# An LSTM cell updated in two halves, and the eigenvector work given out by window length

## The chip, the cores and the metric

The kernel runs on one core of a Trainium2 chip. The metric is the device time of one execution in microseconds; the time before is the median of three runs. The profile is one separately profiled execution of the same program. The engines are named as in the profile: PE (matmuls), PEld (weight loads for PE), DVE (vector), ACT (activations), POOL (general), SP (which here issues most transfers).

## The reference, cut to what matters

Four graph layers run one after the other over `x` of shape (128, 64, 256): 128 batches, 64 nodes, 256 features. After each layer comes a residual and a layer norm. The change concerns the first layer and, through the work that is interleaved with it, the eigenvectors for the fourth.

```python
# layer 0
h = relu(einsum('ts,bsh->bth', adj, x @ Wg0 + bg0))
h = relu(einsum('ts,bsh->bth', adj, h @ Wg1 + bg1))
for p in range(1, 5):
    nw = Tv // p                                   # Tv = 64 nodes
    wins = h[:, :nw * p, :].reshape(Bv * nw, p, Hd)
    last = lstm_last(Wih[p-1], Whh[p-1], bih[p-1], bhh[p-1], wins)
    h = h.at[:, arange(nw) * p + (p - 1), :].set(last.reshape(Bv, nw, Hd))
x = layernorm(x + h)

# one LSTM step, gates in the order i, f, g, o, zero initial state
g = x_t @ Wih.T + h @ Whh.T + bias
c = sigmoid(f) * c + sigmoid(i) * tanh(gg)
h = sigmoid(o) * tanh(c)

# layer 3 needs U
_, U = eigh(L_norm)        # 64x64, from adj
```

Windows of p nodes in a row are run through an LSTM of p steps; the last hidden state replaces the last node of each window. This is done for p = 1, 2, 3 and 4 in turn, each on the result of the one before. The eigenvectors `U` depend on `adj` alone, so they can be computed at any time before layer 3.

## The kernel before, in words

Everything is fp32. In the first layer the batches are split into four groups (`g`), each of 16 tiles of two batches (`TG = 16`). A group's state `H` holds the features on the 128 partitions in two halves (the index `c`), and 2048 columns (two batches by 64 nodes by 16 tiles).

For each group the loop at L1649 runs `windows` for p = 1, 2, 3, 4. In `windows` (L1564) the columns are cut into parts: four for p = 1 (512 columns each), two for p = 2 (512), two for p = 3 (336), one for p = 4 (512). For each part the p steps run in order (`k`). In a step the gates come in the order 0, 1, 3, 2, that is i, f, o, g; f is left out in the first step, when the old cell is zero. Each gate has two chunks `c`, the two halves of the hidden features. A chunk is two matmuls from `H` with the input weights `wi` (L1589) and, from the second step on, two from the hidden state `hst`, tile `lh`, with `wh` (L1593). Both add up in one of four PSUM banks (tag `pq`). ACT then applies the sigmoid or tanh with the bias and writes the chunk into the gate's tile (L1595). In the trace each matmul call is two PE instructions.

Only when all gates are done is the cell updated, on both chunks at once, with operations of 1024 columns (672 for p = 3): the product of i and g at L1605 (L1603 in a first step), the product of the old cell and f at L1606, their sum at L1607, the tanh of the cell on ACT at L1608, and the product with o, which is the new `lh`, at L1611. In the last step the product is written straight into `H` instead, by two strided operations (L1615). The next step's L1593 needs `lh`; the next p needs `H`.

Three kinds of work are interleaved. `side` issues parts of something else on PE: the residual and layer norm of the group before while p is 1 and 2, and the graph convolution of the group after while p is 3 and 4. `pump` issues pieces of the eigenvector computation, mostly chains of tiny DVE operations on 64 rows, a few with 64x64 matmuls. Each call adds an amount of units to what is owed and takes pieces off a generator until it is paid; a piece says what it is worth, 1.1 to 5 units, or 2.6 where it doesn't say. A piece is tied behind the DVE instruction that was written down last, so that it can't be put ahead of it in DVE's queue:

```python
with tc.issue_after(mark[0]):
    while owed[0] > 0:
        owed[0] -= next(pieces, None) or 2.6
```

Within a step `pump` is called after each chunk but the last two (L1597). The amount is 1.2 (a first step) or 2.13 (a later one), times the columns over 512, times `PACE`, 1.9. What is left of the pieces is pumped beside the second layer and must be done before the third begins.

Each engine works through its own queue in order. The order of the queues is set when the program is built: a scheduler takes the instructions by their place in the program and by when it reckons that their operands will be ready, so a queue isn't always in the order of the code. The small matrix `b0w` is made once at the start from a bias, and read by four PE instructions (L1520).

Of the kernel before, what the change touches and what calls it, by code (L numbers as in the profile page):

```python
# [7 lines left out]
F32 = mybir.dt.float32  # L8
I32 = mybir.dt.int32
AF = mybir.ActivationFunctionType  # L10
ALU = mybir.AluOpType
# [6 lines left out]
P = 128  # L18
# [1241 lines left out]
def tile_adj_resnorm(ctx: ExitStack, tc: tile.TileContext, I: dict, out: bass.AP, layers: int = 4):  # L1260
    nc = tc.nc
    v, s, te = nc.vector, nc.scalar, nc.tensor
# [18 lines left out]
    lh = head.enter_context(tc.tile_pool(name="lh", bufs=1, side="right"))  # L1281
# [99 lines left out]
    PACE = 1.9  # L1381

    def pump(n):

        owed[0] += n
        body = nc.cur_bb.bb.instructions
        for i in reversed(body[seen[0] :]):
            if i.engine == mark[0].engine:
                mark[0] = i
                break  # L1390
# [3 lines that stand above are left out]
        seen[0] = len(body)  # L1394
# [84 lines left out]
    with tc.tile_pool(name="lw", bufs=1) as lw, tc.tile_pool(  # L1479
        name="l0c", bufs=1  # L1480
    ) as lc, tc.tile_pool(name="l0p", bufs=2, space=PSUM) as pp, tc.tile_pool(
        name="l0r", bufs=1, space=PSUM
    ) as pr, tc.tile_pool(name="l0q", bufs=4, space=PSUM) as pq:
        G = 4 * D
        TG = 16
# [19 lines left out]


        negc = lw.tile([P, 2, N], F32, tag="negc", name="negc")
        b0w = lw.tile([P, 2, P], F32, tag="b0w", name="b0w")
        rs = lw.tile([P, 1], F32, tag="rs", name="rs")
        ps = pp.tile([P, 512], F32, tag="ps", name="ps")  # L1510
        te.matmul(ps[:, :P], ones, bda, start=True, stop=True)
# [52 lines left out]
        def windows(l0, H, p, w, side):  # L1564


            wi, wh = w
            nw = N // p
            hn = H.rearrange("p c (b n j) -> p c b n j", b=2, j=TG)

            parts = {1: [(b, b + 1, n, n + 32) for b in range(2) for n in (0, 32)], 4: [(0, 2, 0, nw)]}.get(
                p, [(b, b + 1, 0, nw) for b in range(2)])
            for b0, b1, n0, n1 in parts:
                M = (b1 - b0) * (n1 - n0) * TG
                at = lambda c, k: hn[:, c, b0:b1, n0 * p + k : (n1 - 1) * p + k + 1 : p, :]
                cst_ = l0.tile([P, 2, 512], F32, tag="lc", name="lc", bufs=2)
                hst = None
                for k in range(p):
                    gates, left = {}, 8 if k else 6
                    for gt in (0, 1, 3, 2):  # L1580
                        if gt == 1 and k == 0:
                            continue
                        gates[gt] = l0.tile([P, 2, 512], F32, tag="gate", name="gate", bufs=5)
                        for c in range(2):
                            left -= 1
                            o = gt * 2 + c
                            ps = pq.tile([P, 512], F32, tag="pq", name="pq")[:, :M]
                            for kk in range(2):
                                te.matmul(ps, wi[:, kk, o * P : (o + 1) * P], at(kk, k),  # L1589
                                          start=(kk == 0), stop=(k == 0 and kk == 1))  # L1590
                            if k:
                                for kk in range(2):
                                    te.matmul(ps, wh[:, kk, o * P : (o + 1) * P], hst[:, kk, :M],  # L1593
                                              start=False, stop=(kk == 1))
                            s.activation(gates[gt][:, c, :M], ps, AF.Tanh if gt == 2 else AF.Sigmoid,  # L1595
                                         bias=bl[:, p - 1, o : o + 1])
                            if left >= 2:  # L1597
                                pump((0.8 * 6 / 4 if k == 0 else 1.6 * 8 / 6) * M / 512 * PACE)
                            side(M / 512 * (1 if k == 0 else 2))
                    cs2 = cst_[:, :, :M]  # L1600
                    gi, gg, go = (gates[q][:, :, :M] for q in (0, 2, 3))
                    if k == 0:
                        v.tensor_tensor(cs2, gi, gg, ALU.mult)  # L1603
                    else:
                        v.tensor_tensor(gi, gi, gg, ALU.mult)  # L1605
                        v.tensor_tensor(cs2, cs2, gates[1][:, :, :M], ALU.mult)  # L1606
                        v.tensor_tensor(cs2, cs2, gi, ALU.add)  # L1607
                    s.activation(gg, cs2, AF.Tanh)  # L1608
                    if k < p - 1:
                        hst = l0.tile([P, 2, 512], F32, tag="lh", name="lh")  # L1610
                        v.tensor_tensor(hst[:, :, :M], go, gg, ALU.mult)  # L1611
                    else:
                        wb = lambda a, c: a[:, c, :].rearrange("p (b w j) -> p b w j", w=n1 - n0, j=TG)
                        for c in range(2):
                            v.tensor_tensor(at(c, k), wb(go, c), wb(gg, c), ALU.mult)  # L1615

        def residual(g, H, pool, tag):
            hj = H.rearrange("p c (m j) -> p c j m", j=TG)
# [28 lines left out]
        with tc.tile_pool(name="l0g", bufs=1) as l0:  # L1647
            back = iter(())
            for g in range(NT // TG):  # L1649


                side = paced(back, TG // 2, LOAD[1] + LOAD[2] - 4)
                for p in (1, 2):
                    windows(l0, H, p, weights(p), side)
                for _ in back:
                    pass
                last, more = H, iter(())
                if g < NT // TG - 1:
                    if g < NT // TG - 2:
                        load_x(g + 2)  # L1660
                    H = new_h(g + 1)
                    more = convolve(g + 1, H)
                side = paced(more, TG * 2, LOAD[3] + LOAD[4] - 4)
                for p in (3, 4):
                    windows(l0, last, p, weights(p), side)
                for _ in more:
                    pass
                if g < NT // TG - 1:
                    back = residual(g, last, pr, "pr")
# [16 lines left out]
    lw, sm = own2(only1, name="l1w", bufs=1), own2(only1, name="l1s", bufs=2)  # L1686
# [42 lines left out]
    for q in range(NQ):  # L1729
        nc.sync.dma_start(xd[q], xq(q))  # L1730
        at = sm.tile([P, 2, 512], F32, tag="at", name="at")
# [71 lines left out]
    with tc.tile_pool(name="eps3", bufs=1, space=PSUM) as eps:  # L1803
# [7 lines left out]
        with tc.For_i(0, nc.values_load(again[0:1, 0:1], min_val=0, max_val=1)):  # L1811
            with tc.tile_pool(name="gk2", bufs=1) as gk2, tc.tile_pool(name="gt2", bufs=1) as gt2, tc.tile_pool(
                name="gp2", bufs=1, space=PSUM
# [9 lines left out]
    with ExitStack() as l2:  # L1823
# [215 lines left out]
        lw, sm = own1(valuing, name="l2w", bufs=1), own1(valuing, name="l2s", bufs=2)  # L2039
# [17 lines left out]
        with tc.tile_pool(name="l3w", bufs=1) as l3w, tc.tile_pool(name="l3s", bufs=2) as s3, tc.tile_pool(  # L2057
            name="l3p", bufs=6, space=PSUM
# [144 lines left out]
```

## Time and profile before

| what | value |
|---|---|
| median of 3 runs | 2417.96 us (2417.39 to 2418.26) |
| the profiled execution | 2424.67 us |
| its span, first to last instruction | 2422.9 us |
| mean granted PE clock | 0.98 |
| first layer's gate matmuls | from 71.5 us to 1528 us |
| DVE busy in the whole span | 1791.2 us |
| ACT busy in the whole span | 961.6 us |

The span is what the profile accounts for; the execution's own time has 1.8 us more around it, and the profiled execution is 6.7 us above the median of the runs.

A row of the groups reads: line, engine, operation, the tile written and the tiles read, partitions x columns, how often; then the busy time in us and the mean of one in ns; then the idle time of that engine just before these instructions, with what ended it. A matmul's end is modelled and overlaps the next one's start, so a busy PE is not PE at its peak. PEclk is the granted clock as a share of full speed. A line of the timeline begins with its start and its duration in us. A line of the table of stages has the stretch, its length, busy time and number of instructions, the granted clock, and the DMA engines' share and GB/s.

### The profile page before, as it was taken

The numbers are of one execution on the slowest core, as the hardware profiler recorded it, in microseconds if no ns is written. First come the engines' busy times: TensorE is split into PE (matmuls) and PEld (weight loads), VectorE is DVE, ScalarE is ACT, GpSimd is POOL, SyncE is SP. The second block draws the span as 40 slices with busy tenths as digits, with TensorE's granted clock in tenths as the row PEclk, the third lists the DMA queues.
The fourth block names the chain that finished last, engine by engine and source line by source line (L and its number), as shares of the span: only waits on it lengthen the run. The fifth ranks groups of instructions, "written<-read, shape, count | busy, mean of one in ns | idle before, by whom it ended". The sixth has DMA issues, their size and how long they took to land. (4 is left out here: it accounts for less than half of the span.)

```text
span 2422.9 us, 29207 instructions
## 1 busy us (share of the span) xinstructions
PE 2291.4 (95%) x9016; PEld 1228.3 (51%) x9016; DVE 1791.2 (74%) x8172; ACT 961.6 (40%) x1678; POOL 76.2 (3%) x115
## 2 busy tenths in 40 slices
PE   7999999999999999999999989998989999899797
PEld 5544654444565444664444554554433433246786
DVE  4667766677977788867799887687867878457577
ACT  2322322242323242333242322333437875456575
POOL 0000000000000000000000000000000000002331
PEclk9999999999999999999999999999999999899899
DMA  6001000000100010100000100012211000511622
GB/s 217 18 18 35 1 35 1 25 28 18 53 1 35 1 53 18 52 2 34 35 18 18 53 18 18 1 66 87 78 45 35 27 22 26 96 40 43 136 88 75
DMA packets 59859, 101.24 MB, mean 42 GB/s; under 512 B 5136, under 2 KB 40080, under 8 KB 59440
## 3 DMA queue, kind: packets, MB, share of 16 engines
q1 hardware_dynamic: 54624, 88.83, 11.6%
q0 software_dynamic: 3216, 10.21, 1.5%
q8 instruction: 72, 1.18, 0.2%
q14 instruction: 91, 0.75, 0.1%
q10 hardware_dynamic: 1856, 0.28, 0.1%
HBM read 67.84 MB, written 31.46 MB: 41 GB/s over the span
## 5 line engine op out<-in xcount | busy, mean ns | idle before, releaser
L1589 PE MATMUL pq<-H,wi 128*128 128x512 f32 (+1 forms) x2016 | 829.7, 547 | 6.0 <-DVE H L1615 5.1
L1595 ACT ACTIVATE gate<-pq,bl 128x512 f32<-128x512 f32 (+1 forms) x504 | 317.3, 635 | 848.9 <-PE pq L1593 668.6
L1589 PEld LDWEIGHTS pq<-H,wi 128*128 128x128 f32 x2016 | 373.8, 191 | 334.5 <-issue 260.0
L1593 PE MATMUL pq<-lh,wh 128*128 128x512 f32 (+1 forms) x1152 | 477.2, 540 | 25.7 <-DVE lh L1611 25.3
L1593 PEld LDWEIGHTS pq<-lh,wh 128*128 128x128 f32 x1152 | 216.1, 192 | 224.0 <-issue 138.3
L1928 DVE SCALAR_TENSOR_TENSOR xs<-xs 128x512 f32<-128x512 f32 x256 | 165.3, 682 | 64.8 <-ACT xs L1927 63.8
L1927 ACT COPY xs<-l 128x512 f32<-128x512 f32 x256 | 136.7, 586 | 76.0 <-PE l L1920 38.9
L1920 PE MATMUL l<-edge_s,xq 64*128 64x512 f32 x512 | 136.1, 630 | 17.6 <-ACT xs L1927 12.7
L1897 PE MATMUL m<-wqv,xT 128*128 128x512 f32 x256 | 122.7, 616 | 0.8 <-DVE xT L1888 0.8
L1741 PE MATMUL ps<-at,w 128*128 128x512 f32 x256 | 116.7, 607 | 4.1 <-ACT at L1737 3.6
L1759 PE MATMUL ps<-h,w 128*128 128x512 f32 x256 | 113.6, 602 | 6.9 <-ACT h L1754 6.9
L1608 ACT ACTIVATE gate<-lc 128x1024 f32<-128x1024 f32 (+1 forms) x72 | 69.0, 958 | 123.2 <-DVE lc L1603 62.8
L1253 ACT ACTIVATE X<-X,ln_sh,ln_rs 128x256 f32<-128x256 f32 x192 | 99.2, 590 | 19.5 <-DVE ln_sh L1249 13.8
L142 DVE COPY AQR<-eps 64x192 f32<-64x192 f32 (+1 forms) x125 | 35.1, 281 | 94.0 <-PE eps L148 93.9
L1237 DVE BATCH_NORM_STATS2 ln_st<-X 128x6 f32<-128x256 f32 x256 | 99.2, 415 | 2.2
L1605 DVE TENSOR_TENSOR gate<-gate 128x1024 f32<-128x1024 f32 (+1 forms) x36 | 38.0, 1056 | 73.2 <-ACT gate L1595 73.2
L1897 PEld LDWEIGHTS m<-wqv,xT 128*128 128x128 f32 x256 | 46.0, 193 | 77.6 <-issue 62.9
L1759 PEld LDWEIGHTS ps<-h,w 128*128 128x128 f32 x256 | 48.6, 193 | 66.6 <-issue 56.6
L1920 PEld LDWEIGHTS l<-edge_s,xq 64*128 64x128 f32 x512 | 46.4, 190 | 70.0 <-issue 33.0
L1992 POOL DMA_DIRECT2D xr<-xv x32 | 17.6, 549 | 2018.5 <-PE m L1897 1804.3
L1741 PEld LDWEIGHTS ps<-at,w 128*128 128x128 f32 x256 | 47.1, 192 | 60.0 <-issue 47.2
L1874 PE MATMUL sc<-xs,az 128*32 128x512 f32 x512 | 69.1, 612 | 3.1 <-DVE xs L1928 3.1
(556 smaller groups left out, 3217.9 us busy)
## 6 DMA issues: line engine op xcount, KB each, us to landing
wi<-in_WihT_dram SPq DMA_DIRECT2D x16, 1024.0 KB, 4.9
wh<-in_WhhT_dram SPq DMA_DIRECT2D x12, 1024.0 KB, 6.4
X<-in_x_dram SPq DMA_DIRECT2D x16, 512.0 KB, 8.8
xd<-X SPq DMA_DIRECT2D x16, 512.0 KB, 4.0
X<-xd SPq DMA_DIRECT2D x16, 512.0 KB, 3.2
xv<-xv SPq DMA_DIRECT2D x32, 256.0 KB, 2.0
xr<-xv POOLq DMA_DIRECT2D x32, 256.0 KB, 2.9
M<-attn_d SPq DMA_DIRECT2D x16, 512.0 KB, 11.2
```

The lines of the kernel that those rows point to most:

```text
L1237: nc.vector.bn_stats(st, self.X[:, k, :])
L1253: nc.scalar.activation(x, x, AF.Identity, bias=sh[:, k : k + 1], scale=rs[:, k : k + 1])
L1589: te.matmul(ps, wi[:, kk, o * P : (o + 1) * P], at(kk, k), start=(kk == 0), stop=(k == 0 and kk == 1))
L1593: te.matmul(ps, wh[:, kk, o * P : (o + 1) * P], hst[:, kk, :M], start=False, stop=(kk == 1))
L1595: s.activation(gates[gt][:, c, :M], ps, AF.Tanh if gt == 2 else AF.Sigmoid, bias=bl[:, p - 1, o : o + 1])
L1741: te.matmul(ps, w1[:, k, c * P : (c + 1) * P], at[:, k, :], start=(k == 0), stop=(k == 1))
L1759: te.matmul(ps, w2[:, k, c * P : (c + 1) * P], h[:, k, :], start=(k == 0), stop=(k == 3))
L1874: mms.append(te.matmul(sc[half][c][q : q + 32, :], az[:, c, HU - 1 - u_ : 3 * HU - 1 - u_], xs[b, i], start=(u_ == 0), stop=(u_ == HU - 1)))
L1897: te.matmul(ps, xT[:, i, c, :], wqv[:, c, :], start=(c == 0), stop=(c == 1))
L1920: mms.append(te.matmul(pl[i][:, b, :], xq[i][r, c * P : (c + 1) * P], GG[r, :], start=True, stop=True))
L1927: taken.append(s.copy(x, pl[i][:, b, :]))
L1928: ready.append(v.scalar_tensor_tensor(x, x, 0.2, x, ALU.mult, ALU.max))
```

## The change

The cell is updated chunk by chunk inside the loop over gates. After each chunk of gate f the product with the old cell is issued; after each chunk of gate g, which is the last, the product of i and g, the sum, the tanh and, but in the last step, the product into the hidden state. The hidden state's tile is taken at the start of the step and has two buffers. The two operations into `H` stand behind the loop over the steps and are the same as before.

The pump's amount is multiplied by 0.85 for p = 1 and 2, and by 1.1 for p = 3 and 4. `b0w` no longer has a place of its own, but takes that of `h1`, a tile of the convolution.

```diff
-        b0w = lw.tile([P, 2, P], F32, tag="b0w", name="b0w")
+        b0w = lc.tile([P, 2, 512], F32, tag="h1", name="b0w")[:, :, :P]
...
                 for k in range(p):
+                    hnew = l0.tile([P, 2, 512], F32, tag="lh", name="lh", bufs=2) if k < p - 1 else None
                     gates, left = {}, 8 if k else 6
...
                             if left >= 2:
-                                pump((0.8 * 6 / 4 if k == 0 else 1.6 * 8 / 6) * M / 512 * PACE)
+                                pump((0.8 * 6 / 4 if k == 0 else 1.6 * 8 / 6) * M / 512 * PACE * (0.85 if p < 3 else 1.1))
                             side(M / 512 * (1 if k == 0 else 2))
-                    cs2 = cst_[:, :, :M]
-                    gi, gg, go = (gates[q][:, :, :M] for q in (0, 2, 3))
-                    if k == 0:
-                        v.tensor_tensor(cs2, gi, gg, ALU.mult)
-                    else:
-                        v.tensor_tensor(gi, gi, gg, ALU.mult)
-                        v.tensor_tensor(cs2, cs2, gates[1][:, :, :M], ALU.mult)
-                        v.tensor_tensor(cs2, cs2, gi, ALU.add)
-                    s.activation(gg, cs2, AF.Tanh)
-                    if k < p - 1:
-                        hst = l0.tile([P, 2, 512], F32, tag="lh", name="lh")
-                        v.tensor_tensor(hst[:, :, :M], go, gg, ALU.mult)
-                    else:
-                        wb = lambda a, c: a[:, c, :].rearrange("p (b w j) -> p b w j", w=n1 - n0, j=TG)
-                        for c in range(2):
-                            v.tensor_tensor(at(c, k), wb(go, c), wb(gg, c), ALU.mult)
+                            cs, g = cst_[:, c, :M], {q: a[:, c, :M] for q, a in gates.items()}
+                            if gt == 1:
+                                v.tensor_tensor(cs, cs, g[1], ALU.mult)
+                            if gt != 2:
+                                continue
+
+                            if k == 0:
+                                v.tensor_tensor(cs, g[0], g[2], ALU.mult)
+                            else:
+                                v.tensor_tensor(g[0], g[0], g[2], ALU.mult)
+                                v.tensor_tensor(cs, cs, g[0], ALU.add)
+                            s.activation(g[2], cs, AF.Tanh)
+                            if k < p - 1:
+                                v.tensor_tensor(hnew[:, c, :M], g[3], g[2], ALU.mult)
+                    hst = hnew
+
+                wb = lambda a, c: a[:, c, :M].rearrange("p (b w j) -> p b w j", w=n1 - n0, j=TG)
+                for c in range(2):
+                    v.tensor_tensor(at(c, p - 1), wb(gates[3], c), wb(gates[2], c), ALU.mult)
```

## The prediction

> **What bounds the kernel now.** I read the page's first two parts first, then the groups by shape, then the waits of PE, then a table of stages, and last the timeline around one stalled and one unstalled hand-over.
>
> ```profile
> span 2422.9 us, 29207 instructions
> PE 2291.4 (95%) x9016; PEld 1228.3 (51%) x9016; DVE 1791.2 (74%) x8172; ACT 961.6 (40%) x1678; POOL 76.2 (3%) x115
> L1589 PE MATMUL pq<-H,wi 128*128 128x512 f32 (+1 forms) x2016 | 829.7, 547 | 6.0 <-DVE H L1615 5.1
> L1593 PE MATMUL pq<-lh,wh 128*128 128x512 f32 (+1 forms) x1152 | 477.2, 540 | 25.7 <-DVE lh L1611 25.3
> ```
>
> PE is the bound, and 54% of the span is the LSTM's two matmul lines (the stage runs from 71 to 1528 us). The only sizeable idle time before them is 25.3 us waiting for lh, the new hidden state, and 5.1 us waiting for H. So what this change can win in the matmul stage is stalls, not work. The table of stages for groups 2 and 3 (p = 1, 2, 3, 4 each) shows whose lateness it is:
>
> ```profile
> core 0: us, DVE busy (x), PEclk, DMA share, GB/s
> 849.00:892.00 43.00, 37.37 (x184) 1.00 0.12 48
> 892.00:978.00 86.00, 77.93 (x429) 0.96 0.08 26
> 978.00:1095.00 117.00, 87.94 (x457) 0.99 0.12 42
> 1095.00:1206.00 111.00, 82.36 (x448) 1.00 0.02 5
> 1206.00:1248.00 42.00, 37.32 (x193) 1.00 0.12 49
> 1248.00:1334.00 86.00, 77.68 (x438) 0.98 0.07 26
> 1334.00:1431.00 97.00, 83.26 (x374) 1.00 0.11 44
> 1431.00:1528.00 97.00, 73.56 (x490) 0.98 0.04 11
> ```
>
> DVE is 87 to 91% busy while p is 1 or 2, but 74 to 76% at p = 4. Now the hand-over at 1258.9, the first step of p = 2:
>
> ```profile
> 1258.93 0.69 ACT L1595 ACTIVATE gate<-pq,bl 128x512 f32<-128x512 f32 x1 [0.97 <-PE pq L1589]
> 1263.82 1.21 DVE L1603 TENSOR_TENSOR lc<-gate 128x1024 f32<-128x1024 f32 x1
> 1265.06 1.06 ACT L1608 ACTIVATE gate<-lc 128x1024 f32<-128x1024 f32 x1 [5.45 <-DVE lc L1603]
> 1266.15 1.23 DVE L1611 TENSOR_TENSOR lh<-gate 128x1024 f32<-128x1024 f32 x1
> 1267.43 4.97 PE L1593 MATMUL pq<-lh,wh 128*128 128x512 f32 x7 [3.80 <-DVE lh L1611]
> ```
>
> The last gate is done at 1259.62, but DVE starts the cell at 1263.82: 4.2 us of eigenvector pieces (64x1 operations, back to back in the timeline) are in front of it. Then the chain itself takes 3.56 us. PE, which had input matmuls to run meanwhile, waits 3.80 us, and its next seven passes take 4.97 instead of about 3.2 us, because the clock has dropped. The unstalled hand-over at 1171, step 3 of p = 4:
>
> ```profile
> 1171.22 0.69 ACT L1595 ACTIVATE gate<-pq,bl 128x512 f32<-128x512 f32 x1 [4.46 <-PE pq L1593]
> 1171.94 1.23 DVE L1605 TENSOR_TENSOR gate<-gate 128x1024 f32<-128x1024 f32 x1 [3.46 <-ACT gate L1595]
> 1176.08 1.23 DVE L1611 TENSOR_TENSOR lh<-gate 128x1024 f32<-128x1024 f32 x1 [1.18 <-ACT gate L1608]
> 1177.37 2.84 PE L1593 MATMUL pq<-lh,wh 128*128 128x512 f32 x6 [0.17 <-DVE lh L1611]
> ```
>
> Here DVE was idle when the gate came; the chain takes 5.4 us from the gate's end and PE waits 0.17 us: convolution and hoisted input matmuls cover nearly all of it. So a stall needs a late DVE; the chain only sets how much lateness PE forgives.
>
> [...] the trace agrees (1222 ns at 1024, 852 at 672, 682 at 512, 504 at 336 by its groups), so a halved operation costs its fixed part again: 2x0.682-1.22 = 0.14 us. [...] the tanh at 1024 measures 1056[...]. [...] the seven passes above agree, and the clock columns 0.96, 0.98, 0.98 price it at 3.4, 1.7 and 1.9 us.
>
> **The change, part by part.**
>
> *Halved operations.* In one group the extra DVE operations are 4 (p=1), 10 (p=2), 18 (p=3), 13 (p=4): 45, 180 in all. At 0.14 to 0.15 us they are 26 us of DVE time; the 72 tanhs add about 0.17 us each, 12 us of ACT. ACT is 30% busy in this stage. On DVE they lie in its idle time, 1.5 us in p=2 and 2.7 in p=3; if DVE were full there, they would come back as PE wait.
>
> *Shorter chain.* After the last gate's second chunk only its own half remains; the first half and the f-product run beside matmuls (a recurrent chunk is four matmul calls, 8 passes, 3.4 us at 512). From the gate's end to lh: at 512, first step 3.56 -> 0.68+0.61+0.68+0.1 = 2.1; later steps 5.4 -> 3x0.68+0.61+0.15 = 2.8. At 336 2.5 -> 1.5 and 3.4 -> 2.1. So 1.0 to 2.6 us more lateness is forgiven.
>
> *Pace.* Per group the pumps ask 36.5+66.9 units in p=1,2 and 75.8+82.1 in p=3,4 (from the factors in the code). After: 87.9 and 173.7. The total, 261.5 instead of 261.3, is the same, so the later layers receive the same remainder, and the 1% of a piece costs nothing there. From p=1 about 5.5 units go. Pieces are about 23 of the 37.4 us there (the rest being four lc, eight H writes and residual work), 0.65 us a unit: 3.5 us less backlog where DVE was 4.2 us late.
>
> *New order on DVE.* pump ties each piece behind the last DVE instruction written down. The f-products are now such instructions, so the pieces of the following chunks queue behind an f-product that waits for its gate. No row shows this. At best it is a gain (the cell's work cannot be overtaken by later pieces), at worst each of the 36 recurrent steps loses about 2 us of piece time. I take nothing: pieces pumped earlier are there to fill the wait.
>
> *lh in two buffers, b0w in h1's slot.* The second lh buffer is needed since the first half is written while matmuls still read the old state; it takes a wait away. b0w's readers (L1520) end by 11.5 us and the first h1 write is at 16.7: no cost. No DMA moves and no queue is passed.
>
> **The sum**, stage by stage, with the waits for lh that the trace gives in those stretches:
> - p=2: waits 4.8 (group 2) and 5.4 (group 3), half clock 3.4+1.7. Lateness falls by 3.5 and the chain by 1.5, against at most 3.8: I leave 1.3. Gain 14.
> - p=3: waits 5.0, 4.2, 4.2, nine in all, seven above 1 us. The chain returns 1.0 to 1.35 on each, 8. But 7.6 more units come (about 6 us) plus 2.7 of halves onto a DVE that in group 3 is at 83 of 97: I give back 4. Gain 4.
> - p=4: waits 0.2, 0.2, 0.2, 1.2. Gain 1.5.
> - H before p=4 of group 3: 5.1 us, half clock 1.9; the last chain is 1.4 us shorter[...]. Gain 2.5.
> - Start of the next layer: L1741 waits 3.1 us for a copy that stands on ACT behind the last tanh (1532.6). The chain ends 1.5 us sooner. Gain 1.5.
> - Unforeseen order: loss 2.
>
> Gain 21.5 us. The profiled execution took 2424.67 us (span 2422.9), 6.7 above the median of the runs; taken off the median the forecast is 2396 us.
>
> **Rivals.**
> - *Everything goes*: all 32 us of waits, 7 of slow clock, 3 at the layer's start: 42, so 2376. For it: p=4 shows that a DVE in time leaves 0.2 us. Against: p=3 gets more DVE work.
> - *Given back at p=3,4*: DVE, relieved in p=1,2, is full in p=3, and as much is lost there as was won. For it: group 3's 83.26 us becomes about 92 of 97. Against: the shorter chain. About 2414.
> - *Slower*: pieces held behind the f-products make DVE late at every recurrent step. Place: L1593 of p=3 and p=4. Price: 36 steps, half of them 2 us late at PE (36), a slow-clock window of 1.7 in five (8), less the 21.5 that remains: +22, so 2440. It decides once DVE passes about 95% in p=3. Against: 26% of DVE is idle in p=4 now.
> - *No change*: the scheduler places the first half's work behind the second's gates, and the chain is as long as before; then the pace alone acts, and wins and losses cancel: 2418.
>
> **How the numbers follow.** Forecast 0.58 (2384 to 2408), everything goes 0.12, given back 0.12, no change 0.04, slower 0.14. The range for 8 in 10 is 2376 to 2416. Within 0.2% (5 us, about what a measurement of this kernel can tell) are part of "given back" and "no change". Faster 0.78, same 0.07, slower 0.15.
>
> **What would show it.** Right: waits for lh under 12 us in total; PEclk 1.00 in both p=2 stretches; the cell's first operation there under 1 us late; tanh at 512 near 0.61 us; L1593 ends near 1508. Wrong: lh waits of p=3 above 14 us, or DVE above 95% there; waits of ACT for DVE at the first half's tanh that hold up the second half's gate.

## The result and the profile after

The changed kernel takes 2413.19 us (median of 20 runs, 2408.29 to 2417.51) and the kernel before 2419.01 us (20 runs, 2415.90 to 2423.11). The ratio is 0.9975, with a 95% interval of 0.9969 to 0.9981: 5.8 us faster, where 21.5 were forecast. The direction is right, the size is not.

The profiled execution of the changed kernel took 2413.07 us (span 2411.2), 0.1 us off its median. That of before took 2424.67 us, longer than any of its 20 timed runs. Differences between the two profiles are therefore larger than the difference of the medians. A second profile of the unchanged kernel (run e0_before below) stands beside the first for that reason.

The page of the kernel after, first part and groups (idle time before a group, and what ended most of it, come last in a line):

```profile
span 2411.2 us, 29498 instructions
PE 2289.0 (95%) x9016; PEld 1226.7 (51%) x9016; DVE 1815.5 (75%) x8352; ACT 974.3 (40%) x1750; POOL 76.4 (3%) x115
L1590 PE MATMUL pq<-H,wi 128*128 128x512 f32 (+1 forms) x2016 | 836.4, 547 | 6.1 <-DVE H L1619 4.0
L1594 PE MATMUL pq<-lh,wh 128*128 128x512 f32 (+1 forms) x1152 | 481.8, 534 | 16.0 <-DVE lh L1614 12.7
```

The costs came out as forecast: 180 more DVE instructions and 24.3 us more of DVE (26 forecast), 72 more on ACT and 12.7 us (12 forecast). The wait for lh fell from 25.3 to 12.7 us, just over the 12 forecast. Yet all idle time before these two lines is 16.0 and 6.1 us, 3.3 and 2.1 more than lh and H account for; before, that remainder was 0.4 and 0.9. The waits of PE, after (total, times, longest):

```profile
PE pq L1594 <- DVE lh L1614: 12.7, 16, 2.7
PE pq L1590 <- DVE H L1619: 4.0, 1, 4.0
PE ps L1745 <- ACT at L1741: 3.2, 2, 3.0
PE eps L148 <- DVE dg L124: 2.0, 1, 2.0
PE pq L1590 <- ACT gate L1596: 1.7, 1, 1.7
PE pq L1594 <- DVE rq_a L126: 1.5, 1, 1.5
PE pq L1594 <- DVE qb L124: 1.0, 1, 1.0
```

Three things show. The wait at the start of the next layer (L1745, 3.0 us) is as long as it was before, where the line read:

```profile
PE ps L1741 <- ACT at L1737: 3.6, 3, 3.1
```

PE now waits for a gate on ACT (L1596). And it waits for single operations of the eigenvector pieces (dg, rq_a, qb).

The table of stages for groups 2 and 3 (p = 1, 2, 3, 4 each, PE, PEld, DVE, ACT and POOL busy in this order):

```profile
core 0: us, PE busy (x) PEld busy (x) DVE busy (x) ACT busy (x) POOL busy (x), PEclk, DMA share, GB/s
844.00:887.00 43.00, 43.00 (x111) 19.80 (x110) 35.94 (x183) 19.69 (x31) 0.00 (x0) 1.00 0.13 48
887.00:970.00 83.00, 79.43 (x196) 35.83 (x195) 72.56 (x376) 28.84 (x42) 0.00 (x0) 0.98 0.07 27
...
1195.00:1237.00 42.00, 42.00 (x109) 19.27 (x108) 34.65 (x178) 19.22 (x31) 0.00 (x0) 1.00 0.12 47
1237.00:1320.00 83.00, 79.19 (x199) 35.76 (x199) 73.31 (x389) 29.27 (x43) 0.00 (x0) 1.00 0.08 27
1320.00:1416.00 96.00, 87.77 (x305) 57.24 (x304) 86.82 (x445) 31.76 (x60) 0.00 (x0) 0.99 0.12 43
1416.00:1515.00 99.00, 96.71 (x223) 41.85 (x222) 83.67 (x514) 23.68 (x36) 0.00 (x0) 0.98 0.04 11
```

The p = 2 stretches are 3 us shorter each, 83 instead of 86, and still not full on PE. Group 3's p = 4 is 2 us longer than before, 99 instead of 97.

To compare runs by stretch I use PE's lost time: the length of a stretch less its matmuls at the pitch they keep when nothing stalls (in the trace of the kernel after 429 ns at 512 columns, 19 of L1590 in the 8.15 us from 849.47; 282 at 336, 20 in the 5.65 us from 970.33). Each entry is worked out from the trace of one execution, and is good to about 1 us, since the pitch of the small 64-row matmuls in between has to be chosen. The columns are before and e0_before, after, e1_pace, e2_cell, e3_tanh and e11_tanh_fprod, which are described below. The wait for H, which ends p = 3 of group 3, is in the p = 3 row.

| lost time of PE, us | before, two profiles | after | pace alone | cell alone | after, tanh order mended | after, both mends |
|---|---|---|---|---|---|---|
| p=2, groups 2 and 3 | 16.1, 16.0 | 11.1 | 6.7 | 15.9 | 3.5 | 3.5 |
| p=3, groups 1 to 3 | 27.6, 25.9 | 17.9 | 19.7 | 18.7 | 18.8 | 19.3 |
| p=4, groups 1 to 3 | 5.6, 5.6 | 8.8 | 6.8 | 5.3 | 8.7 | 3.5 |
| whole LSTM stage | 108.1, 104.5 | 94.8 | 89.0 | 99.4 | 88.5 | 85.6 |
| median of the runs | 2419.0 | 2413.2 | 2406.7 | 2412.6 | 2405.4 | 2399.8 |

### The profile page after: what moved, and what is told of

Its sections match the earlier page's. It is cut to its first block, busy times and chain, and to the rows that moved or that the text cites. A ratio compares the mean times of both kernels' runs of the same rounds, so it can differ in the third digit from the quotient of the medians.

```text
span 2411.2 us, 29498 instructions
## 1 busy us (share of the span) xinstructions
PE 2289.0 (95%) x9016; PEld 1226.7 (51%) x9016; DVE 1815.5 (75%) x8352; ACT 974.3 (40%) x1750; POOL 76.4 (3%) x115
## 3 DMA queue, kind: packets, MB, share of 16 engines
q1 hardware_dynamic: 54624, 88.83, 11.6%
## 5 line engine op out<-in xcount | busy, mean ns | idle before, releaser
L1590 PE MATMUL pq<-H,wi 128*128 128x512 f32 (+1 forms) x2016 | 836.4, 547 | 6.1 <-DVE H L1619 4.0
L1596 ACT ACTIVATE gate<-pq,bl 128x512 f32<-128x512 f32 (+1 forms) x504 | 317.6, 635 | 791.0 <-PE pq L1594 642.3
L1590 PEld LDWEIGHTS pq<-H,wi 128*128 128x128 f32 x2016 | 371.9, 191 | 331.0 <-issue 256.7
L1594 PE MATMUL pq<-lh,wh 128*128 128x512 f32 (+1 forms) x1152 | 481.8, 534 | 16.0 <-DVE lh L1614 12.7
L1612 ACT ACTIVATE gate<-lc 128x512 f32<-128x512 f32 (+1 forms) x144 | 83.5, 580 | 166.6 <-DVE lc L1608 80.9
L1745 PE MATMUL ps<-at,w 128*128 128x512 f32 x256 | 116.7, 607 | 3.8 <-ACT at L1741 3.2
L1610 DVE TENSOR_TENSOR gate<-gate 128x512 f32<-128x512 f32 (+1 forms) x72 | 43.4, 603 | 45.9 <-ACT gate L1596 45.3
L1745 PEld LDWEIGHTS ps<-at,w 128*128 128x128 f32 x256 | 47.2, 192 | 59.7 <-issue 46.8
```

What stands on the lines that cost most here:

```text
L1590: te.matmul(ps, wi[:, kk, o * P : (o + 1) * P], at(kk, k), start=(kk == 0), stop=(k == 0 and kk == 1))
L1745: te.matmul(ps, w1[:, k, c * P : (c + 1) * P], at[:, k, :], start=(k == 0), stop=(k == 1))
```

## Where the chain went

The hand-over that the prediction worked with, the first step of p = 2 in group 3, now in the timeline of the kernel after:

```profile
1245.74 0.69 ACT L1596 ACTIVATE gate<-pq,bl 128x512 f32<-128x512 f32 x1 [1.03 <-PE pq L1590]
1249.73 0.68 DVE L1608 TENSOR_TENSOR lc<-gate 128x512 f32<-128x512 f32 x1
1250.44 0.63 ACT L1612 ACTIVATE gate<-lc 128x512 f32<-128x512 f32 x1 [4.02 <-DVE lc L1608]
1250.98 0.67 ACT L1596 ACTIVATE gate<-pq,bl 128x512 f32<-128x512 f32 x1
1251.14 0.68 DVE L1614 TENSOR_TENSOR lh<-gate 128x512 f32<-128x512 f32 x1
1251.75 0.68 DVE L1608 TENSOR_TENSOR lc<-gate 128x512 f32<-128x512 f32 x1
1251.88 1.12 PE L1594 MATMUL pq<-lh,wh 128*128 128x512 f32 x2 [2.75 <-DVE lh L1614]
1252.46 0.63 ACT L1612 ACTIVATE gate<-lc 128x512 f32<-128x512 f32 x1 [0.81 <-DVE lc L1608]
1253.12 0.69 DVE L1614 TENSOR_TENSOR lh<-gate 128x512 f32<-128x512 f32 x1 [0.70 <-ACT gate L1612]
1253.87 1.12 PE L1594 MATMUL pq<-lh,wh 128*128 128x512 f32 x2 [0.42 <-DVE lh L1614]
```

The second half's gate had its matmuls at 1247.4 (one chunk, 1.72 us, after the first half's). It starts at 1250.98, 3.6 us late: the first half's tanh stands ahead of it in ACT's queue, waiting for a DVE that is 3.3 us late. With the gate put ahead of the tanh (e3_tanh below) it starts 0.04 us after its matmuls. So the second half begins at 1251.75, though the first half's product was done at 1250.41; tanh, gate, product, tanh, product follow one another. From DVE's start to lh it is 1253.81-1249.73 = 4.1 us, where the undivided cell of before took 3.56.

A hand-over for which DVE was in time, p = 4 of group 2 in the same trace:

```profile
1160.19 0.69 ACT L1596 ACTIVATE gate<-pq,bl 128x512 f32<-128x512 f32 x1 [2.29 <-PE pq L1594]
1160.91 0.69 DVE L1610 TENSOR_TENSOR gate<-gate 128x512 f32<-128x512 f32 x1 [2.29 <-ACT gate L1596]
1161.63 0.69 DVE L1611 TENSOR_TENSOR lc<-lc,gate 128x512 f32<-128x512 f32 x1
1162.42 0.63 ACT L1612 ACTIVATE gate<-lc 128x512 f32<-128x512 f32 x1 [1.54 <-DVE lc L1611]
1163.08 0.69 DVE L1614 TENSOR_TENSOR lh<-gate 128x512 f32<-128x512 f32 x1 [0.15 <-ACT gate L1612]
```

From the gate's end (1160.88) to lh (1163.77) it is 2.9 us, against 2.8 forecast and 5.4 before. The halved chain is short where DVE is in time, and there PE waited 0.17 us before the change. Where DVE is late, at the places with something to win, it isn't.

## The experiments

Each kernel is an edit of the kernel before or of the changed one. Those measured together share the runs of before, whose medians are 2419.70 (e0 to e3), 2419.75 (e4 to e7) and 2420.49 us (e8 to e11).

**e0_before.** The kernel before, unedited.

> The kernel before once more, for a second profile of it. The profiled execution of before (2424.67 us) lies above its 20 runs (median 2419.0), that of after (2413.07) at its median. If the 13.3 us by which the LSTM stage is shorter in the two traces are partly chance of one execution, this profile has fewer stalls before L1593: waits for lh about 20 us instead of 25.3, and the stage ends near 1522. If the stalls are the program's own, it shows 25 us again and the end near 1528.

2423.27 us profiled; waits for lh again 25.3 us in 17 places, lost time 104.5 against 108.1. The stalls belong to the program and not to one execution. The 3.6 between them are mostly two windows of 3.4 us at half clock (PEclk 0.50), at 83 us in group 0 and 691 us in group 1, that the first profile has and the second hasn't (1.7 us each).

**e1_pace.** The kernel before with the new pace and nothing else.

```diff
-pump((0.8 * 6 / 4 if k == 0 else 1.6 * 8 / 6) * M / 512 * PACE)
+pump((0.8 * 6 / 4 if k == 0 else 1.6 * 8 / 6) * M / 512 * PACE * (0.85 if p < 3 else 1.1))
```

> The kernel before with the new factors of the pump alone (0.85 and 1.1). If the pace is what won the time at p = 2, this has most of the gain: about 2413 us, the first cell operation of p = 2 late by under 3 us. If the gain came from the halved cell, this is the kernel before, 2419 us, or slower, since p = 3 gets 10% more pieces with the long chain: 2422.

2406.69 us, ratio 0.9950 (0.9937 to 0.9964). Two numbers alone are 13 us faster, more than the whole change, whose interval doesn't touch this one. DVE's lateness at the first step of p = 2 falls from 3.6 to 2.7 us in group 2 and from 4.2 to 1.8 in group 3.

**e2_cell.** The changed kernel with the old pace.

```diff
-... * M / 512 * PACE * (0.85 if p < 3 else 1.1))
+... * M / 512 * PACE)
```

> The halved cell with the old pace. Theory A (the first half's tanh stands in ACT's queue ahead of the second half's gate, so that a late DVE delays that gate too): with 15% more pieces in p = 1 and 2 the stalls there are at least as long as before, 2417 to 2420 us. Theory B (DVE's lateness alone counts, the chain is shorter): each late hand-over is 1.5 us shorter, 2410 us.

2412.58 us, ratio 0.9965 (0.9952 to 0.9978). Each part wins, 13 and 7 us, but together only 5.8. On top of the new pace, the cell as it is written costs about 6 us (2413.2 against 2406.7). The second buffer of `lh` and `b0w`'s new place belong to it here and weren't tried apart; the stage's first matmul comes at 71.4 us, at 71.5 before, so `b0w` holds nothing up that shows. The table above shows where: p = 2, 6.7 us lost by pace alone and 11.1 in the changed kernel.

**e3_tanh.** The changed kernel, with both tanhs behind the second half's gate and both lh products behind them. `ga` is that gate's activation; the dependency puts the first tanh behind it in ACT's order.

```diff
-                            s.activation(g[2], cs, AF.Tanh)
+                            if c == 0:
+                                continue
+                            for q in range(2):
+                                t = s.activation(gates[2][:, q, :M], cst_[:, q, :M], AF.Tanh)
+                                if q == 0:
+                                    tc.add_manual_dep(
+                                        t.ins, ga.ins.name,
...
                             if k < p - 1:
-                                v.tensor_tensor(hnew[:, c, :M], g[3], g[2], ALU.mult)
+                                for q in range(2):
+                                    v.tensor_tensor(hnew[:, q, :M], gates[3][:, q, :M], gates[2][:, q, :M], ALU.mult)
```

> The changed kernel with one more edge: on ACT the tanh of the first half stands behind the activation of the second half's gate. In the trace of after that activation starts up to 3.6 us after its matmuls at the stalled hand-overs (0.04 us where DVE is in time). Theory A: it starts within 0.3 us now, the late hand-overs of p = 2 and 3 are 1 to 1.5 us shorter and spare a slow-clock stretch, waits for lh fall from 12.7 to about 6 us, 2405 us. Theory B: no difference, 2413 us.

2405.38 us, ratio 0.9935 (0.9922 to 0.9948): this edit was worth 8 us. It has the same 180 additional DVE instructions and 72 tanhs as the changed kernel, so these alone are not what makes that one slower than pace alone. Against pace alone (2406.69) it is only 1.3 us faster, which the intervals don't tell apart. The same hand-over in its timeline:

```profile
1239.81 0.69 ACT L1596 ACTIVATE gate<-pq,bl 128x512 f32<-128x512 f32 x1 [1.03 <-PE pq L1590]
1241.47 0.68 DVE L1608 TENSOR_TENSOR lc<-gate 128x512 f32<-128x512 f32 x1
1241.53 0.69 ACT L1596 ACTIVATE gate<-pq,bl 128x512 f32<-128x512 f32 x1 [1.03 <-PE pq L1590]
1242.18 0.63 ACT L1615 ACTIVATE gate<-lc 128x512 f32<-128x512 f32 x1
1242.88 0.68 DVE L1608 TENSOR_TENSOR lc<-gate 128x512 f32<-128x512 f32 x1
1243.49 1.47 DVE L1623 TENSOR_TENSOR lh<-gate 128x512 f32<-128x512 f32 x2
1243.60 0.63 ACT L1615 ACTIVATE gate<-lc 128x512 f32<-128x512 f32 x1 [0.79 <-DVE lc L1608]
1244.22 1.98 PE L1594 MATMUL pq<-lh,wh 128*128 128x512 f32 x4 [0.67 <-DVE lh L1623]
```

The gate starts when its matmuls are done (1241.53), and PE waits 0.67 us instead of 2.75. DVE is also less late here, 1.0 us after the first half's gate where it was 3.3. This can be followed back through p = 1 of group 3 (DVE's delay at a window's first cell operation, counted from the first half's gate; the delay of the second gate behind its matmuls). The last two rows are the same pair of kernels with the old pace, e2_cell and e4_tanh_oldpace:

| us | window 1 | 2 | 3 | 4 | p=2, step 1 |
|---|---|---|---|---|---|
| DVE late, after | 0.82 | 1.78 | 2.36 | 2.38 | 3.31 |
| gate late, after | 1.08 | 2.03 | 2.62 | 2.64 | 3.56 |
| DVE late, e3_tanh | 0.92 | 0.78 | 0.46 | 0.03 | 0.97 |
| gate late, e3_tanh | 0.04 | 0.04 | 0.04 | 0.04 | 0.04 |
| DVE late, e2_cell | 0.80 | 1.36 | 2.23 | 2.66 | 3.12 |
| DVE late, e4_tanh_oldpace | 0.79 | 1.55 | 2.50 | 3.31 | 3.41 |

With the new pace the order keeps DVE in time; with the old one DVE falls behind as far with it as without it, so the order of ACT is not the only thing that makes DVE late. In the changed kernel a DVE that is 3.31 us late delays a tanh, the tanh a gate by 3.56 us, and DVE stands idle for what this gate leads to. Its idle time before the two operations that follow a tanh, by its groups at 512 columns, first of the kernel after:

```profile
L1619 DVE TENSOR_TENSOR H<-gate 128x512 f32<-128x512 f32 x56 | 38.7, 691 | 24.9 <-ACT gate L1612 23.8 <-PE pq L1590 0.8
L1614 DVE TENSOR_TENSOR lh<-gate 128x512 f32<-128x512 f32 x40 | 27.5, 688 | 15.1 <-ACT gate L1612 14.8
```

and of e3_tanh:

```profile
L1628 DVE TENSOR_TENSOR H<-gate 128x512 f32<-128x512 f32 x56 | 38.2, 682 | 8.2 <-ACT gate L1615 7.4
L1623 DVE TENSOR_TENSOR lh<-gate 128x512 f32<-128x512 f32 x40 | 27.4, 685 | 6.6 <-ACT gate L1615 6.0
```

40.0 us of idle DVE become 14.8. Most of that only moves: before the first operations of a half (L1608 and L1610, 512 columns) DVE's idle time rises from 39.5 to 56.7 us. In the stretches of p = 1 and 2 of groups 2 and 3, all of DVE's idle time together falls from 35.2 to 27.1 us. The edit moves the lh products with the tanhs, so the two are not told apart by it.

**e4_tanh_oldpace.** e3_tanh with the old pace, to see whether the order is worth the same without the new one.

> The halved cell with the two tanhs behind the second half's gate on ACT, and the pieces paced as in the kernel before. If the ACT order costs its microseconds whatever the pace is, this gains on e2_cell (2412.6 us, waits for lh 20.0 us) about what the order gained under the new pace (7.8 us): 2405 us, waits for lh 13 to 15 us. If the order only matters together with the new pace (because the late DVE of p = 3 is what holds the tanh up), little is gained over e2_cell: 2410 to 2413 us, waits for lh 18 us or more.

2413.52 us, ratio 0.9971 (0.9964 to 0.9979); waits for lh 21.1 us. Nothing is gained over e2_cell. The lost time at p = 2 falls a little (15.9 to 13.5), but p = 3 of groups 2 and 3 rises from 11.8 to 17.8. Waits for lh are 2.1 us of this rise, half clock another 2.1. With this order the first half of lh comes only after both gates, which would lengthen the waits when DVE is late; the runs don't show that cause apart. At p = 1 of group 3 DVE was idle for 5.1 us in e2_cell and is for 4.6 here (7.9 and 6.0 with the new pace), so there was little for the order to win. So the 8 us are the order's worth under the new pace, not a price for itself.

**e5_tanh_flat.** e3_tanh with 1.0 in place of 1.1.

```diff
-... * PACE * (0.85 if p < 3 else 1.1))
+... * PACE * (0.85 if p < 3 else 1.0))
```

> e3_tanh with the factor for p = 3 and 4 put back from 1.1 to 1.0, so that about 15 units a group of eigenvector pieces are left for the later layers. If the extra pieces of p = 3 and 4 are what fills DVE in group 3, the time that PE loses there (11.1 us at p = 3, 7.7 at p = 4 in e3_tanh) falls to about 7 and 4, and with nothing lost later the run takes 2398 us. If the pieces left over are paid for in the layers after the LSTM, the stage is as short but the run takes 2405 us or more.

2425.37 us, ratio 1.0017 (1.0009 to 1.0025), although the LSTM stage lost only 79.9 us, 8.6 less than in e3_tanh. The waits of PE in this run show where it went:

```profile
PE ps L1754 <- ACT at L1750: 12.6, 3, 6.8
...
PE eps L148 <- DVE dg L124: 11.3, 2, 6.4
...
PE eps L183 <- DVE delta L124: 6.2, 1, 6.2
...
PE eps L183 <- DVE V L129: 3.6, 1, 3.6
```

The pieces that were left over come after the stage. The start of the next layer waits 12.6 us instead of 3.2. Of the waits before the pieces' own matmuls (L148 for dg, L183), 14.8 us lie between 1790 and 1800 us, where e3_tanh has no such wait; the other one for dg, 6.4 us at 1669, stands where PE waits 6.9 us for ACT in e3_tanh, and so is no loss. PE is also at half clock for 103 us after the stage, against 76. The run is 20 us longer than e3_tanh, so the 8.6 us won in the stage cost nearly 29 after it.

**e6_tanh_steep.** e3_tanh with factors 0.7, 0.7, 1.0, 1.25 for p = 1 to 4.

> e3_tanh with factors 0.7, 0.7, 1.0 and 1.25 for p = 1 to 4 (72.4+75.8+102.6 = 250.8 units a group in place of 261.5). If pieces cost nothing wherever DVE is idle on average (p = 4, 74 to 76% busy before), the loss at p = 2 goes to under 1 us, at p = 3 of group 3 to about 7, p = 4 stays: 2400 us. If p = 4 has no room in its stretches without convolution, group 3's p = 4 loses more than its 7.7 us and the run is no faster than e3_tanh, 2405 us.

2409.54 us, ratio 0.9960 (0.9945 to 0.9975). The stage is the best of all, 74.1 us lost (p = 2: 1.7, p = 3 of group 3: 4.8), but dg, delta and the next layer's start wait 11.3, 7.1 and 6.4 us. The same waits as in e5_tanh_flat come back, with 10.7 units a group fewer than in e3_tanh.

**e7_fprod.** The changed kernel, with the forget product of each half behind the product of i and g.

```diff
-                            if gt == 1:
-                                v.tensor_tensor(cs, cs, g[1], ALU.mult)
...
                                 v.tensor_tensor(g[0], g[0], g[2], ALU.mult)
+                                v.tensor_tensor(cs, cs, g[1], ALU.mult)
                                 v.tensor_tensor(cs, cs, g[0], ALU.add)
```

> The changed kernel with the forget product of each half written down after the product of input and candidate, behind the last gate, so that no piece queues behind a forget product that waits for its gate. If the forget products hold pieces back and make DVE late, this is faster than the changed kernel: 2408 us or less. If they only take 0.5 to 0.7 us off the chain of each half, moving them behind the last gate lengthens the chain of 36 recurrent steps, half of which are late at PE: 2413 + 18 x 0.6 = 2424 us; with the first half's product still beside matmuls, half of that, 2418 us. Between: 2413 us, where the forget product is of no weight either way.

2408.95 us, ratio 0.9956 (0.9939 to 0.9973), 4 us better than the changed kernel; the two intervals just overlap. It isn't the wait that the prediction feared: forget products waited 2.5 us for their gates in the whole kernel after. 3.6 of the stage's 4.5 us are in group 3's p = 4, where the timeline of the kernel after has this:

```profile
1481.90 0.23 DVE L124 TENSOR_SCALAR dg<-cst,dcol 64x32 f32<-64x32 f32 x1
1482.05 0.21 DVE L117 TENSOR_TENSOR Z<-za,zb 64x1 f32<-64x1 f32 x2
1482.18 0.30 PE L148 MATMUL eps<-dg,cst 64*64 64x32 f32 x2 [2.02 <-DVE dg L124]
1482.41 1.12 PE L1594 MATMUL pq<-lh,wh 128*128 128x512 f32 x2
```

A matmul of the eigenvector pieces stands in PE's queue between recurrent matmuls that are ready, and waits 2.02 us for a piece on DVE. In e7_fprod dg is ready 1.0 us before PE takes it, and nobody waits:

```profile
1474.15 0.23 DVE L124 TENSOR_SCALAR dg<-cst,dcol 64x32 f32<-64x32 f32 x1
1475.38 0.30 PE L148 MATMUL eps<-dg,cst 64*64 64x32 f32 x2
```

The edit moved where the scheduler put this pair. That is 2.0 of the 3.6 us. Another 1.2 are half clock: behind the wait for H, the first 5.2 us of this stretch are at half clock in the kernel after, 2.8 in e7_fprod. This lies 60 us ahead of the pair and isn't its doing.

**e8_tanh_138.** e3_tanh with factors 0.7, 0.7, 1.0, 1.38, as many units in total as the changed kernel.

> e3_tanh with factors 0.7, 0.7, 1.0, 1.38 for p = 1 to 4: 72.4+75.8+113.3 = 261.5 units a group, as many as the changed kernel asks, so nothing more is left for the later layers. If e6_tanh_steep was held up by its leftovers alone, its shorter LSTM stage (PE's lost time 74.1 us against 88.5 in e3_tanh) comes through, less about 4 us for the larger pace in the last group's p = 4: 2395 us. If p = 4 can't take the pieces, the last group's p = 4 loses over 10 us and the run is at 2405 us.

2406.02 us, ratio 0.9941 (0.9929 to 0.9954). The leftover is gone (no wait for dg), but p = 4 can't take that many pieces: it loses 5.9, 5.5 and 7.8 us in groups 1 to 3, against 0.5, 0.5 and 7.7 in e3_tanh. What p = 2 and 3 win, p = 4 gives back.

**e9_all_138.** e8_tanh_138 with e7_fprod's edit.

> e8_tanh_138 with the forget products behind the last gate, as in e7_fprod. If an early forget product holds pieces back where DVE is in time (e7_fprod's gain of 3.6 us was all in the last group's p = 4), the denser pieces of p = 4 make this gain at least as large here: 4 us under e8_tanh_138, 2391 us. If the longer chain of this form counts instead, it is 2 us above e8_tanh_138.

2405.87 us, ratio 0.9939 (0.9925 to 0.9953): no difference to e8_tanh_138, where 4 us were expected. With this pace dg held nothing up before the edit. So the early forget products have no price that comes back in another pace. What can be pointed to of e7_fprod's gain is one matmul pair that fell well, 2.0 us, and less half clock in the profiled execution.

**e10_pace_138.** The kernel before with 0.7, 0.7, 1.0, 1.38.

> The kernel before with the factors 0.7, 0.7, 1.0, 1.38 and nothing else. If pace is what wins and the halved cell is worth nothing on top of it, this is within 3 us of e8_tanh_138, about 2396 us. If the halved cell with its tanhs in order forgives 1 to 2.5 us of lateness at each step, this one is slower than e8_tanh_138 by as much as e3_tanh's p = 2 and p = 3 stretches beat e1_pace's (some 6 us): 2401 us.

2415.73 us, ratio 0.9980 (0.9973 to 0.9987), slower than both expectations. Its p = 4 loses 8.2, 8.6 and 8.4 us. Compared with e8_tanh_138 the halved cell with its tanhs in order is worth 9.7 us here. The forecast gave the shorter chain almost nothing to do at p = 4; it has something, once the pace makes DVE late there.

**e11_tanh_fprod.** The changed kernel's pace with the edits of e3_tanh and e7_fprod.

> The changed kernel's pace with both mends: the tanhs behind the second half's gate (e3_tanh) and the forget products behind the last gate (e7_fprod). If they are two separate costs, their gains add: 2413.2 - 7.8 - 4.2 = 2401 us, and PE's lost time in the last group's p = 4 falls from e3_tanh's 7.7 us to about 3. If they are one cost seen twice, this stays at 2405 us.

2399.81 us, ratio 0.9919 (0.9905 to 0.9934). The two gains add (2401 expected), group 3's p = 4 loses 2.5 us instead of 7.7, and dg holds nobody up. Of these 5.2 us, 2.0 are the wait for dg that e3_tanh has too and 2.8 half clock, of which 1.7 are in a window that opens 0.9 us after that wait. It is 13 us faster than the changed kernel and the fastest version here, 7 us ahead of pace alone:

```profile
PE pq L1594 <- DVE lh L1622: 10.7, 11, 1.9
...
PE pq L1590 <- DVE H L1627: 4.3, 1, 4.3
...
PE ps L1753 <- ACT at L1749: 3.2, 2, 3.0
```

H and the next layer's start remain as they were.

## Why the prediction was right in direction and wrong in size

**p = 2, gain 14: the step that failed.** The prediction added two terms for the hand-over at p = 2: lateness down by 3.5 us and a chain shorter by 1.5. Counted from the end that the last gate had, or would have had if not held up, lh was there 7.8 us later before (4.2+3.56), 2.8 later in the forecast (0.7+2.1), and 5.7 later in the kernel after (1.6+4.1). Of 5.0 us, 2.1 came. The term that failed is the shorter chain, with 2.0 of the 2.9 us that are missing: it grew from 3.56 to 4.1 us instead of falling to 2.1, since the first half's tanh held up the second half's gate. The term for the lateness was too large by the other 0.9, 3.5 us where 2.6 came; pace alone, which blocks no gate, gave 2.4. The lost time fell by 5.0 us instead of 14, and by less than pace alone took off (9.4). With the order mended, lh comes 2.7 us after the gate, and the two stretches gain 12.6. So the forecast's size was that of a kernel whose second gate is not held up. It named the danger in its last line (ACT at the first half's tanh holding up the second half's gate) and put no price on it: none of its rivals is that case. Its 14 also holds 5.1 us of half clock. In the traces PEclk is 0.50 for 6.8 us in group 2 and 3.4 us in group 3 before, and for 3.4 us in group 2 alone after: by the clock 5.1 us lost, and 1.7.

**p = 3, p = 4 and H, gain 4 + 1.5 + 2.5: nearly right in sum, not in parts.** p = 3, with the wait for H, lost 27.6 us and now 17.9, 9.7 less (8.0 by the second profile), although group 3 has DVE busy for 86.82 of 96 us. The forecast had counted 8.7 us more of DVE there (its 6 us for 7.6 units would be 4.9 at its own 0.65 us a unit); 3.6 came. p = 4 loses 3.2 more. There, 2.2 of group 3's 6.4 us are in front of eigenvector matmuls, which the forecast didn't look at. The wait for H fell only from 5.1 to 4.0, and PEclk at its end is 0.50 for 6.8 us where it was for 3.4. Of the 2.5 us forecast there, 1.4 are the shorter chain; the other 1.1, off the 1.9 us of half clock, were the author's estimate, and the traces don't show them. Together 6.5 of 8. "Given back at p = 3, 4" is the rival whose time, 2414, came nearest, but not its mechanism: p = 3 won, and p = 2 fell short.

**Next layer's start, gain 1.5: nothing.** 3.1 us before, 3.0 after. The last tanh did end 1.0 us sooner, 3.4 us after the last matmul instead of 4.4. But the copy (L1741) followed the tanh at once before, and after it starts 0.8 us behind it; the trace gives the last product into `H` (L1619) as what it waited for.

**The base.** The measured terms add up to 5.0+6.5+0.1 = 11.6 us, and 11.6 lie between the two profiled executions (2424.67 and 2413.07). That these are equal is in part chance: the whole stage lost 13.3 us less, 1.8 of it in stretches that no term names, and what follows the stage took 1.6 longer. The forecast took its gain, read from a profile 6.7 us above the median, off the median. The median fell by 5.8, half of what the profiles differ by. So of the 15.7 us by which the gain was overrated, 9.0 are the hand-over at p = 2, about 6 the distance between profiles and medians, and the remaining 0.9 what the smaller terms leave together.

**Pace and cell apart.** Pace was priced through 3.5 us less backlog at two places, and the rival in which it acts alone was set at 2418. Alone it gave 2406.7. At p = 2, where the forecast put two thirds of its gain, the halved cell alone won next to nothing (15.9 us lost, 16.1 before). So the direction there comes from the pace, the forecast's first term; the second, a chain that forgives more, came to nothing until the tanhs were in order. That a total of 261.5 units instead of 261.3 leaves the later layers as they are was right and mattered more than thought: e5_tanh_flat shows what 15.8 units a group too few cost.

**What held.** The number and the price of the halved operations: tanh 629 and 483 ns at 512 and 336 columns, where a straight line through the means of before, 1056 ns at 1024 and 763 at 672, gives 630 and 483; the 0.61 us at 512 in the forecast's chain was the author's estimate. The slower rival, pieces held behind waiting forget products, isn't in the runs (e7_fprod, e9_all_138). PEclk is 1.00 in one p = 2 stretch, 0.98 in the other. The other signs of being right were missed: 12.7 us of waits for lh instead of under 12, 3.3 us of lateness instead of under 1, the stage's end at 1514.9 instead of 1508. Of the signs of being wrong only the last came, ACT's wait at the first half's tanh. The time lies within the range given for 8 in 10, and 5 us outside the forecast's own.

**What stays open.** The profiled execution of before is 5.7 us above its median of 20 runs, the second one 3.6. Half clock explains little of it. The mean granted clock of every run is on record, and 78 runs of before, timed beside the experiments, average 2424.1 us at 0.979 (20 runs), 2420.4 at 0.980 (21) and 2418.3 at 0.981 (30). 0.002 of 2420 us are 4.8, and 5.8 lie between the first average and the last, so most of what separates these runs goes with the granted clock. But both profiles have 0.980, and 2424.67 is longer than any run at that clock (2423.9 at most). What else the median run is spared can't be seen, since only profiled executions have a trace. Also open is how e3_tanh's gain divides between the order on ACT and the products of lh that moved with it, and why that order gains nothing with the old pace beyond what the p = 1 and p = 3 stretches show.

## What to carry to other kernels

When a chain is cut in halves so that the first runs beside the second's producer, look at each engine whose queue holds operations of both. Here it was ACT: with DVE 3.31 us late, the first half's tanh kept the second half's gate 3.56 us behind its matmuls, against 0.04 us with the gate in front (DVE then 0.97 us late), and the overlap was lost just where it was needed. Price such a cut at the late case (4.1 us from DVE's start to lh here), not at the case in time (2.9 us from the gate's end). Filler work could be moved between the stretches here, but its total before the stage's end was owed: 10.7 or 15.8 units a group fewer brought the stage's lost time from 88.5 us to 74.1 or 79.9, and the run from 2405.4 us to 2409.5 or 2425.4.

## What the runs showed that was not expected

With the new pace, over four windows of p = 1 and one step of p = 2 in group 3, the second gate's delay grew from 1.08 to 3.56 us; with the gate first it stayed at 0.04, and DVE stayed under 1 us late. With the old pace the same order left DVE 3.4 us late, and the kernel no faster. And the placing of a single matmul pair of 0.30 us in PE's queue made a wait of 2.02 us, and none where it fell elsewhere.
